# Graph layers in one kernel: a tile's own part of its mean added on TensorE, and eighteen instead of sixteen tiles that gather values together with keys

## The chip, the cores and the metric

The kernel runs on one core of one Trainium2 chip. A core has five engines with their own instruction streams: PE (TensorE: matrix products, which go to PSUM), DVE (VectorE), ACT (ScalarE), POOL (GpSimd) and SP (SyncE, which here only starts transfers). They meet through semaphores. Transfers that pick rows by a list of indices ("gathers") and transfers that write rows to listed places ("scatters") are issued by POOL; each picks one row of DRAM per partition. The metric is the device time of the whole kernel in microseconds.

## The reference

Two graph layers over 4096 nodes with 512 features and an adjacency matrix of 4096 x 4096 (about 0.2% ones, the diagonal set). Each layer is applied to the rectified layernorm of `x` and added to `x`:

```python
# layer 0: per head, the value of the neighbour with the highest score (hard attention)
attn = einsum('hqd,hkd->hqk', Q, K) * SCALING + (Q @ we.T + be)
attn = softmax(attn + where(adj > 0, 0, -inf))
hard = (attn == max(attn)) / HEADS
x = x + einsum('hqk,hkd->hqd', hard, V)
# layer 1: own part and mean over the neighbours
h = relu(layernorm(x))
agg = (adj > 0) @ h / max(deg, 1)
self_f, nb_f = h @ W_self + b_self, agg @ W_nb + b_nb
x = x + relu(concat([self_f, nb_f]) @ W_comb + b_comb)
```

A node is usually its own neighbour, so its own row is a part of the mean of layer 1: the row's product `h @ (W_nb W_comb)`, divided by the degree.

## The kernel before, in words

The rows are cut into 32 tiles of 128. The first part (to about 360 us) reads the adjacency, packs it into lists of neighbours, computes keys and values of all rows into one DRAM table `K_d` (a row holds value, key, meta data and x), and sorts the rows by degree; `perm` holds the order. After that tile 0 has the rows of highest degree (`CAPS[0]` = 24 neighbours) and tile 31 those of lowest (5).

The second part, the turns, goes over the tiles once. Two kinds of tile differ in how they get the values:

- an *apart* tile (`r < VTILE`) gathers only its neighbours' keys, into buffers `kg` (groups of four, four buffers), scores them on DVE (`scores`, a multiplication L1224 and a reduction L1227 for each group), finds the winner of each of the eight heads, and two or three turns later gathers the eight winning value pieces (`value_gathers`, 8 gathers, into `o`);
- a *fused* tile gathers key and value of a neighbour in one row twice as wide, into the big buffer `room`, and then takes the winning values out of `room` with one predicated copy for each neighbour (L1260).

The first group of `scores` is the row's own key, which came with its meta data. `room` is one region: `others(r)` gives the offset of a tile's neighbours, which is 0 for all fused tiles but two of the last four. The other half of `room` holds five slots for rows of fused tiles that fetch their whole own row (`wide`).

The order of turns is worked out by a small planner: four apart tiles first, the last three fused tiles last, and between them fused and apart tiles are mixed evenly. With `VTILE` = 16 these middle 25 turns are 13 fused and 12 apart tiles, which alternate strictly. The planner also fixes in which turn each later step of a tile is done: its values, its statistics (sum with x, L1289, and the normalisation on ACT, L1296 to L1323), its transposition, its two products on PE (`layer1`: `pg`, with the folded neighbour weights, and `pr`, with the folded own weights and the bias) and its move (`layer1_move`: `pg` to `gs` on ACT, L1360; `scatter` of `gs` to `G_d`). Five tiles are done at the end (`tail`) after the last turn.

All is issued in the order in which the loop over the turns writes it, each engine in order. In turn i POOL has: gathers of keys for turn i and values that are due, by turns, one of each; the row gather for turn i+5; the own values (if not wide); the scatter. ACT has: `layer1_move`, the copy of the query's transpose for turn i+2, the copy of the transpose for layer 1 (L1341), statistics, the query's norm for turn i+4, later the norm of layer 1. PE has: the query's product `q` for turn i+1 (L628), `layer1`, transpositions. On DVE `scores` calls `within` after the first gathered group: it takes a reciprocal (L1312) for the statistics that are under way, and does `layer1_out`: own row of the mean times reciprocal plus own product, a `scalar_tensor_tensor` (L1366), which SP stores to `X1_d`.

The third part sums the neighbours' rows of `G_d` (gathers into `room` and a reduction L1674 for 24 tiles; masks and matmuls L1652 for the 8 tiles of highest degree) and scatters the result to the output.

Of the kernel before, what the change touches and what calls it, by code (L numbers as in the profile page):

```python
# [9 lines left out]
F32 = mybir.dt.float32  # L10
BF16 = mybir.dt.bfloat16
I32 = mybir.dt.int32
AF = mybir.ActivationFunctionType
# [5 lines left out]
P = 128  # L19
D = 512  # L20
NC = D // P
H = 8
# [472 lines left out]
LIST = 24  # L495
# [4 lines left out]
M_DEG = 2 * LIST  # L500
M_LN = M_DEG + 1
M_RD = M_LN + 2
# [6 lines left out]
CAPS = (24, 15, 14, 13, 12, 12, 12, 11, 11, 11, 10, 10, 10, 10, 9, 9,  # L509
        9, 9, 9, 8, 8, 8, 8, 8, 7, 7, 7, 7, 6, 6, 6, 5)  # L510
GRP = 4
VTILE = 16
LISTV = CAPS[VTILE]
FIRST = 4
GMAX = 10
# [22 lines left out]
def sparse_path(  # L538
# [4 lines left out]
    nc = tc.nc  # L543
    N = x.shape[0]
    KT = N // P
# [8 lines left out]
    X1_d = dram.tile([N, 2, D], F32, tag="X1_d", name="X1_d")  # L554

    cp = ctx.enter_context(tc.tile_pool(name="sconst", bufs=1))
    ident = cp.tile([P, P], F32, tag="sid", name="sid")
    make_identity(nc, ident)
    identb = cp.tile([P, P], BF16, tag="sidb", name="sidb")
    beb = cp.tile([P, 1], F32, tag="sbe", name="sbe")  # L560
    hio = cp.tile([P, H], F32, tag="hio", name="hio")
    nc.gpsimd.iota(hio, [[1, H]], base=0, channel_multiplier=0, allow_small_or_imprecise_dtypes=True)
# [13 lines left out]
    smeta = cp.tile([P, KT, 8], F32, tag="smeta", name="smeta")  # L576
# [31 lines left out]
    def load_fold(k):  # L608
        nc.sync.dma_start(
            F[:, ds(2 * k * NC, NC), :],  # L610
            (wselfT, wnbT)[k].rearrange("(c p) f -> p c f", p=P),
        )
        nc.sync.dma_start(
            F[:, ds((2 * k + 1) * NC, NC), :],
            wcomb[ts(k, D), :].rearrange("(c p) f -> p c f", p=P),
        )
# [3 lines left out]
    def load_w(name, w, tag):  # L620
        t = wp.tile([P, NC, D], F32, tag=tag, name=name)
        nc.sync.dma_start(t, w.rearrange("(c p) f -> p c f", p=P))
        ws[name] = t


    def project(dst, h, w):
        for c in range(NC):
            nc.tensor.matmul(dst, h[:, c, :], w[:, c, :], start=(c == 0), stop=(c == NC - 1))  # L628

    with ExitStack() as pa:  # L630
        pa.enter_context(tc.manual_schedule())
        lp = pa.enter_context(tc.tile_pool(name="sl", bufs=1))
# [9 lines left out]
        st = [dict() for _ in range(KT)]  # L642
# [42 lines left out]
        load_adj(1)  # L685
        load_w("wv", wvT, "w_b")

        nc.vector.tensor_copy(identb, ident)

        planes = lp.tile([P, NPL, P], BF16, tag="planes", name="planes")  # L690
# [135 lines left out]
        def values(t, ps):  # L826
            pv = ps.tile([P, D], F32, tag="pm", name="pv")
            project(pv, hT(t), ws["wv"])
            return pv
# [100 lines left out]
        def on(step, t, *args):  # L930
            if 0 <= t < KT:
                step(t, *args)
# [159 lines left out]
    with ExitStack() as pb:  # L1092
        gp = pb.enter_context(tc.tile_pool(name="sg", bufs=4))
        bp = pb.enter_context(tc.tile_pool(name="sb", bufs=2))
# [37 lines left out]
        puts, last = [], [None]  # L1132
# [9 lines left out]
        st = [dict() for _ in range(KT)]  # L1142
# [75 lines left out]
        def scores(r, within):  # L1218

            s = st[r]  # L1220
            sc = bp.tile([P, LIST, H], F32, tag="sc", name="sc", bufs=1)
            for kk, g0, g in s["kg"]:
                pr = bp.tile([P, GRP, D], F32, tag="pr", name="pr", bufs=1)
                nc.vector.tensor_tensor(  # L1224
                    pr[:, :g, :], s["q"].unsqueeze(1).to_broadcast([P, g, D]), kk, ALU.mult
                )
                nc.vector.tensor_reduce(  # L1227
                    sc[:, g0 : g0 + g, :],
                    pr[:, :g, :].rearrange("p g (h d) -> p g h d", h=H), AX.X, ALU.add,
                )  # L1230
                if g0:
                    within()
                    within = lambda: None
            s["sc"] = sc
# [108 lines left out]
        def layer1(r):  # L1343
            s = st[r]
            s["pg"] = psm.tile([P, D], F32, tag="pm", name="pg")
            project(s["pg"], s["hT1"], wN)
            s["pr"] = own_product(s)

        def own_product(s):

            pr = psm.tile([P, D], F32, tag="pm", name="pr")
            nc.tensor.matmul(pr, ones[0:1, :], bb[0:1, :], start=True, stop=False)
            for c in range(NC):
                nc.tensor.matmul(pr, s["hT1"][:, c, :], wS[:, c, :], start=False, stop=(c == NC - 1))  # L1354
            return pr

        def layer1_move(r):
            s = st[r]
            s["gs"] = bp.tile([P, D], F32, tag="gs", name="gs")
            nc.scalar.copy(s["gs"], s["pg"])  # L1360

        def layer1_out(r):
            s = st[r]

            own = bp.tile([P, D], F32, tag="own", name="own")
            nc.vector.scalar_tensor_tensor(  # L1366
                own, s["gs"], smeta[:, r, M_RD + 1 - M_DEG : M_RD + 2 - M_DEG], s["pr"],
                ALU.mult, ALU.add,
            )
            nc.sync.dma_start(X1_d[ts(r, P), 1, :], own)  # L1370
# [6 lines left out]
        def load_bias():  # L1377
            for k in range(2):
                fb = bp.tile([P, D], F32, tag="own", name="fb")
                for c in range(NC):  # L1380
                    nc.vector.tensor_copy(
                        fb[:, ts(c, P)], bcs[k][:, c : c + 1].to_broadcast([P, P])
                    )
                fbs.append(fb)
# [47 lines left out]

        fused, apart = list(range(VTILE, KT)), list(range(VTILE))
        turns = apart[:FIRST]
# [23 lines left out]
        for r in turns:  # L1458
            p = pos[r]
# [7 lines left out]
        i = 0  # L1467
        while ready:
            ripe = sorted(e for e in ready if e[0] <= i)
            for e in ripe[: 2 if i >= KT - 4 else 1]:  # L1470
                ready.remove(e)
                r = e[2]
# [15 lines left out]
        def late(step, kind, i, *args):  # L1488

            out_ = []  # L1490
            for r in turns:
                if plan[kind].get(r) == i:
                    out_ += step(r, *args) or []
            return out_

        def tail_turn(r):

            k = tail.index(r)
            at = HALF_R + TAIL0 + k * D
            st[r]["hT1"] = room[:, at : at + D].rearrange("p (c q) -> p c q", q=P)  # L1500
            nc.scalar.copy(st[r]["hT1"], st[r]["hnp"])
# [15 lines left out]
        for i in range(-5, KT):  # L1517


            if i == -3:  # L1520
                load_fold(0)
            if i == 0:
                load_bias()
            if i == 1:
                wS = wp.tile([P, NC, D], F32, tag="w_b", name="swS")
                wN = bp.tile([P, NC, D], F32, tag="swN", name="swN", bufs=1)
            a, b = on(key_gathers, i), late(value_gathers, "value", i)
            while a or b:
                for q, n in ((a, max(1, round(len(a) / max(1, len(b))))), (b, 1)):
                    for g in q[:n]:  # L1530
                        gather(*g)
                    del q[:n]
            on(rows, i + 5)
            late(layer1_move, "move", i)
            on(query_copy, i + 2)
            late(layer1_copy, "layer1", i)
            early = [r for r in tail if plan["turn"][r] == i - 1]
            for r in early:
                tail_turn(r)
            if i >= 0 and turns[i] in fused:  # L1540
                own_values(turns[i])
            late(layer1_stats, "stats", i, i >= KT - 2)
            if i >= KT - 2:
                late(layer1_norm, "stats", i)
            on(query_norm, i + 4)
            on(query, i + 1)
            for part in between.get(i, ()):
                fold(*part)
            late(layer1, "layer1", i)
            for r in early:  # L1550
                tail_product(r)
            if i in (-2, -1, 0):
                n = 2
                for t in late_v[:n]:
                    w = values_out(t, values(t, psm), bp, nc.sync)
                    for g in beyond:
                        tc.declare_no_dep(w.ins, g.ins, reason="other columns")
                    written.append(w)
                del late_v[:n]
            if i == max(between) + 1:  # L1560
                fold_bias()

            def within():
                if i < KT - 2:
                    late(layer1_inverse, "stats", i)
                late(layer1_out, "move", i)

            if i >= 0:
                scores(turns[i], within)
            late(scatter, "move", i)  # L1570
            if i == KT - 2:
                wg = dense_words()
                gsl = [gp.tile([P, GRP, D], F32, tag="kg", name="gs") for _ in range(2)]
            on(winners, i)
            if i < KT - 2:
                late(layer1_norm, "stats", i)
            on(query_turn, i + 3)
            late(layer1_turn, "turn", i)
            for r in early:
                tail_move(r)  # L1580
# [10 lines left out]
            tail_move(r)  # L1591


        over = bp.tile([P, KT], F32, tag="over", name="over", bufs=1)
        r = 0
        while r < KT:
            e = r
# [5 lines left out]
            r = e  # L1603
# [11 lines left out]
        for r in tail:  # L1615
            s = st[r]
# [4 lines left out]
    with ExitStack() as pd:  # L1621
# [78 lines left out]
        s = ahead  # L1700
# [74 lines left out]
```

## Time and profile before

| | |
|---|---|
| median of 3 timed runs | 1424.04 us (1422.22 to 1430.38) |
| the profiled execution | 1295.04 us, span 1293.3 us |
| mean granted TensorE clock in it | 0.899 |
| first turn's scores begin on DVE | 362.8 us |
| last predicated copies begin on DVE | 966.3 us |
| last scatter to `G_d` | 985.7 us |
| DVE sums of `layer1_out` (L1366) | 32, 23.4 us, 733 ns each |
| predicated copies (L1260) | 102, 74.5 us, 731 ns each |
| value gathers into `o` by `vi` (POOL) | 128, 121.9 us, 952 ns each |

The columns of a timeline are the start in us, the duration in us, the engine, the line, the operation, what it writes and reads, how many instructions are merged into one row, and in brackets how long the engine was idle before and what ended that. In a table of stretches each engine has its busy time and, in brackets, its instructions; the last three columns are the granted TensorE clock, the share of DMA engines that were busy and the rate in GB/s. An instruction that only issues a transfer ends long before its data have landed.

### The profile page before, as it was taken

The numbers are of one execution on the slowest core, as the hardware profiler recorded it, in microseconds if no ns is written. First come the engines' busy times: TensorE is split into PE (matmuls) and PEld (weight loads), VectorE is DVE, ScalarE is ACT, GpSimd is POOL, SyncE is SP. The second block draws the span as 40 slices with busy tenths as digits, with TensorE's granted clock in tenths as the row PEclk, the third lists the DMA queues.
The fourth block names the chain that finished last, engine by engine and source line by source line (L and its number), as shares of the span: only waits on it lengthen the run. The fifth ranks groups of instructions, "written<-read, shape, count | busy, mean of one in ns | idle before, by whom it ended". The sixth has DMA issues, their size and how long they took to land.

```text
span 1293.3 us, 10762 instructions
## 1 busy us (share of the span) xinstructions
PE 1025.0 (79%) x2918; PEld 483.8 (37%) x2918; DVE 993.5 (77%) x1666; ACT 422.1 (33%) x862; POOL 776.3 (60%) x910
## 2 busy tenths in 40 slices
PE   5998998958779547767877887878798599999960
PEld 2555555523334213323333333333333244444420
DVE  5557777798279776889988889888792469788876
ACT  4778676831221222343434334344410000000000
POOL 2322323234477777777777777777553757777774
PEclk9999998988898868887889988988898799999985
DMA  9999998739585568888888888887753998888873
GB/s 358 419 421 420 418 420 306 274 133 379 194 253 165 157 186 238 270 265 263 262 264 257 256 249 264 262 246 240 270 187 119 307 356 274 281 271 274 279 248 119
DMA packets 109222, 350.09 MB, mean 271 GB/s; under 512 B 18064, under 2 KB 18064, under 8 KB 100960
## 3 DMA queue, kind: packets, MB, share of 16 engines
q0 software_dynamic: 63376, 208.23, 50.6%
q1 hardware_dynamic: 39552, 129.78, 25.9%
q10 hardware_dynamic: 6224, 11.31, 2.5%
q8 instruction: 25, 0.41, 0.1%
q14 instruction: 45, 0.37, 0.1%
HBM read 285.25 MB, written 68.19 MB: 273 GB/s over the span
## 4 chain that ended last, share of the span: by engine, by line
DVE 21%; DMA 21%; PE 20%; POOL 19%; issue 14%; ACT 3%; SPq 0%; DVEq 0%; POOLq 0%; ACTq 0%
POOL room L1103 9%; PE pv L628 6%; DMA room<-K_d,sidx 6%; DVE pr L1224 6%; DMA room<-G_d,sidx 5%; PE pk L628 5%; POOL kg L1103 5%; DMA kg<-K_d,sidx 4%; POOL o L1103 3%; DVE sc L1227 3%; PE pr L1354 2%; PE pw L768 2%; DMA adjt<-adj_dram 2%; ACT mkt L749 2%; PE pg L628 2%
## 5 line engine op out<-in xcount | busy, mean ns | idle before, releaser
L628 PE MATMUL q<-wq,hqT 128*128 128x512 f32 x256 | 161.2, 788 | 143.0 <-DVE pr L1224 143.0
L1652 PE MATMUL da<-gk,mk 128*128 128x512 f32 x512 | 221.4, 595 | 15.8 <-DMA gk<-G_d 15.8
L1103 POOL DMA_INDIRECT room<-G_d,sidx x174 | 180.3, 1036 | 58.0 <-issue 46.3
L1103 POOL DMA_INDIRECT kg<-K_d,sidx x177 | 169.6, 958 | 57.7 <-issue 45.0
L1227 DVE TENSOR_REDUCE sc<-pr 128x32 f32<-128x2048 f32 (+3 forms) x114 | 183.3, 1608 | 3.9
L1674 DVE TENSOR_REDUCE acc<-room 128x512 f32<-128x4096 f32 (+5 forms) x23 | 152.6, 6634 | 14.0 <-DMA room<-G_d,sidx 14.0
L1652 PEld LDWEIGHTS da<-gk,mk 128*128 128x128 f32 x512 | 97.8, 191 | 139.4 <-issue 139.0
L1103 POOL DMA_INDIRECT o<-K_d,vi x128 | 121.9, 952 | 39.0 <-issue 36.3
L628 PEld LDWEIGHTS q<-wq,hqT 128*128 128x128 f32 x256 | 62.5, 256 | 221.1 <-DVE pr L1224 124.2
L628 PE MATMUL pk<-wk,room 128*128 128x512 f32 x256 | 120.7, 616 | 3.6 <-ACT room L810 3.6
L1103 POOL DMA_INDIRECT room<-K_d,sidx x102 | 98.5, 966 | 31.5 <-issue 18.0
L628 PE MATMUL pv<-wv,room 128*128 128x512 f32 x256 | 115.9, 604 | 0.0
L1224 DVE TENSOR_TENSOR pr<-q,kg 128x2048 f32<-128x2048 f32 (+3 forms) x51 | 102.4, 2007 | 16.0 <-DMA kg<-K_d,sidx 14.4
L1224 DVE TENSOR_TENSOR pr<-q,room 128x2048 f32<-128x2048 f32 (+3 forms) x42 | 66.7, 1589 | 50.8 <-DMA room<-K_d,sidx 42.1
L1354 PE MATMUL pr<-swS,hT 128*128 128x512 f32 x216 | 99.9, 605 | 0.0
L628 PE MATMUL pg<-swN,hT 128*128 128x512 f32 x216 | 97.1, 592 | 0.0
L1296 ACT ACTIVATE hn<-xo 128x512 f32<-128x512 f32 x29 | 18.2, 629 | 192.6 <-DVE xo L1289 185.3
L824 POOL DMA_DIRECT2D K_d<-ks x32 | 18.7, 585 | 100.9 <-DVE ks L819 98.7
L749 ACT ACTIVATE mkt<-adjt,sgb 128x2048 bf16<-128x2048 int32 x37 | 74.2, 2006 | 13.1 <-POOL adjt L670 13.1
L1260 DVE COPY_PREDICATED o<-best,room 128x512 f32<-128x512 int32 x102 | 74.5, 731 | 3.5
L628 PEld LDWEIGHTS pv<-wv,room 128*128 128x128 f32 x256 | 49.6, 195 | 61.4 <-issue 61.2
L628 PEld LDWEIGHTS pk<-wk,room 128*128 128x128 f32 x256 | 48.3, 199 | 54.4 <-issue 48.8
(222 smaller groups left out, 1496.3 us busy)
## 6 DMA issues: line engine op xcount, KB each, us to landing
adjt<-adj_dram SPq DMA_DIRECT2D x37, 1024.0 KB, 11.2
room<-adj_dram SPq DMA_DIRECT2D x27, 1024.0 KB, 11.7
x<-X_d SPq DMA_DIRECT2D x32, 512.0 KB, 6.1
xt<-x_dram SPq DMA_DIRECT2D x32, 256.0 KB, 8.5
K_d<-ks POOLq DMA_DIRECT2D x32, 256.0 KB, 6.4
X_d<-xo SPq DMA_DIRECT2D x32, 256.0 KB, 4.0
X_d<-own SPq DMA_DIRECT2D x32, 256.0 KB, 3.9
gk<-G_d ACTq DMA_DIRECT2D x16, 512.0 KB, 6.0
```

Source lines behind the costliest of these rows:

```text
L628: nc.tensor.matmul(dst, h[:, c, :], w[:, c, :], start=(c == 0), stop=(c == NC - 1))
L749: nc.scalar.activation(mk, st[t]["adj"][j], AF.Sigmoid, bias=sgb, scale=400.0, accum_out=degs[:, t, j : j + 1],)
L768: nc.tensor.matmul(pw, planes[:, s, :], st[t]["mk"][j][:, ts(i, SEG)], start=False, stop=(s == NPL - 1),)
L824: nc.gpsimd.dma_start(K_d[ts(t, P), D : 2 * D], ks)
L1103: last[0] = nc.gpsimd.indirect_dma_start(out=dst, out_offset=None, in_=src, in_offset=bass.IndirectOffsetOnAxis(ap=idx, axis=0), element_o ...
L1224: nc.vector.tensor_tensor(pr[:, :g, :], s["q"].unsqueeze(1).to_broadcast([P, g, D]), kk, ALU.mult)
L1227: nc.vector.tensor_reduce(sc[:, g0 : g0 + g, :], pr[:, :g, :].rearrange("p g (h d) -> p g h d", h=H), AX.X, ALU.add,)
L1260: nc.vector.copy_predicated(s["o"].rearrange("p (h d) -> p h d", h=H), best[:, k, :].bitcast(I32).unsqueeze(2).to_broadcast([P, H, HD]), b ...
L1296: nc.scalar.activation(junk, xo, AF.Copy, scale=-1.0 / D, accum_out=q[:, 0:1])
L1354: nc.tensor.matmul(pr, s["hT1"][:, c, :], wS[:, c, :], start=False, stop=(c == NC - 1))
L1652: nc.tensor.matmul(dacc[r], masks[s][:, h, r, :], keys[s][:, h, :], start=(s == 0 and h == 0), stop=(s == NPL - 1 and h == 1),)
L1674: nc.vector.tensor_reduce(acc, g[:, 0:n, :].rearrange("p n f -> p f n"), AX.X, ALU.add)
```

## The change

For 27 of the 32 tiles the own part of the mean is no longer added on DVE. ACT makes a diagonal matrix `dg` (128 x 128) of the reciprocals of the degrees, by scaling the identity with one number per partition; PE multiplies `dg` with `gs` and adds the product to the group `pr`, which is left open for that; ACT copies the finished sum out of PSUM, and SP stores it. The five tiles of the end keep the sum on DVE. The diagonal and the matmul are done in the turn of the tile's move: `dg` on ACT after the copy of the transpose and ahead of the statistics, the matmul on PE ahead of `q`, the copy on ACT after the scores. `dg` has one buffer.

`VTILE` is 14 instead of 16: tiles 14 and 15 (nine neighbours with the row itself) become fused. The middle 25 turns are then 15 fused and 10 apart tiles, in the order (from turn 5) 14, 5, 15, 16, 6, 17, 7, 18, 19, 8, 20, 9, 21, 22, 10, 23, 11, 24, 25, 12, 26, 13, 27; before it was 16, 5, 17, 6, 18, 7, 19, 8, and so on to 15, 27.

The bf16 identity moves to a pool that is freed after the first part, and the buffer `over` of the last check takes the place of the scores `sc`.

```diff
-VTILE = 16
+VTILE = 14
...
-            s["pr"] = own_product(s)
+            s["pr"] = own_product(s, False)
...
-        def own_product(s):
+        def own_product(s, last=True):
             pr = psm.tile([P, D], F32, tag="pm", name="pr")
             nc.tensor.matmul(pr, ones[0:1, :], bb[0:1, :], start=True, stop=False)
             for c in range(NC):
-                nc.tensor.matmul(pr, s["hT1"][:, c, :], wS[:, c, :], start=False, stop=(c == NC - 1))
+                nc.tensor.matmul(
+                    pr, s["hT1"][:, c, :], wS[:, c, :], start=False, stop=last and c == NC - 1
+                )
             return pr
...
+        def layer1_diag(r):
+            s = st[r]
+            s["dg"] = bp.tile([P, P], F32, tag="dg", name="dg", bufs=1)
+            nc.scalar.activation(
+                s["dg"], ident, AF.Copy, scale=smeta[:, r, M_RD + 1 - M_DEG : M_RD + 2 - M_DEG]
+            )
+
+        def layer1_mean(r):
+            s = st[r]
+            nc.tensor.matmul(s["pr"], s["dg"], s["gs"], start=False, stop=True)
+
+        def layer1_own(r):
+            s = st[r]
+            own = bp.tile([P, D], F32, tag="own", name="own")
+            nc.scalar.copy(own, s["pr"])
+            nc.sync.dma_start(X1_d[ts(r, P), 1, :], own)
...
             for r in early:
                 tail_turn(r)
+            late(layer1_diag, "move", i)
             if i >= 0 and turns[i] in fused:
                 own_values(turns[i])
             late(layer1_stats, "stats", i, i >= KT - 2)
...
             on(query_norm, i + 4)
+            late(layer1_mean, "move", i)
             on(query, i + 1)
...
                     late(layer1_inverse, "stats", i)
-                late(layer1_out, "move", i)
 
             if i >= 0:
                 scores(turns[i], within)
+            late(layer1_own, "move", i)
             late(scatter, "move", i)
...
-        over = bp.tile([P, KT], F32, tag="over", name="over", bufs=1)
+        over = bp.tile([P, LIST, H], F32, tag="sc", name="over", bufs=1).rearrange(
+            "p s h -> p (s h)"
+        )[:, 0:KT]
```

More of the change, by code (lines that the diff above doesn't have):

```diff
@@ L558, in sparse_path @@
     make_identity(nc, ident)
-    identb = cp.tile([P, P], BF16, tag="sidb", name="sidb")
     beb = cp.tile([P, 1], F32, tag="sbe", name="sbe")
@@ L686, in sparse_path @@
         load_w("wv", wvT, "w_b")
+        identb = lp.tile([P, P], BF16, tag="sidb", name="sidb")
         nc.vector.tensor_copy(identb, ident)
```

## The prediction

> **What bounds the kernel now.** I read the page's busy table first, then the engines by stretch of time, then the timelines of POOL and DVE, last the chain that ended last.
>
> ```profile
> PE 1025.0 (79%) x2918; PEld 483.8 (37%) x2918; DVE 993.5 (77%) x1666; ACT 422.1 (33%) x862; POOL 776.3 (60%) x910
> ...
> 600.00:720.00 120.00, 90.61 (x220) 39.94 (x220) 109.87 (x135) 47.09 (x122) 90.79 (x95) 0.87 0.84 262
> 720.00:840.00 120.00, 100.16 (x249) 43.80 (x249) 106.35 (x136) 47.14 (x122) 91.19 (x95) 0.91 0.82 258
> ```
>
> No engine is full over the span. The change lives in the turns, 360 to 960 us. There (columns: PE, PEld, DVE, ACT, POOL busy) POOL looks 76% busy, but it issued 95 instructions in 120 us: 1.26 us from start to start, which is what a gather costs (0.95 busy, 0.31 "issue"). POOL never pauses from 380 to 880 us: it sets the pace. DVE, at 90%, is next.
>
> ```profile
> 610.11 0.95 POOL L1103 DMA_INDIRECT room<-K_d,sidx  x1 [0.30 <-issue]
> ...
> 615.13 0.99 POOL L1119 DMA_INDIRECT G_d<-gs,perm  x1 [0.30 <-issue]
> ...
> 616.25 1.75 DVE L1224 TENSOR_TENSOR pr<-q,room 128x1536 f32<-128x1536 f32 x1
> 616.42 0.97 POOL L1103 DMA_INDIRECT kg<-K_d,sidx  x1 [0.30 <-issue]
> ...
> 620.71 5.33 DVE L1260 COPY_PREDICATED o<-best,room 128x512 f32<-128x512 int32 x7
> ```
>
> Turn 11, a fused one: its last key gather starts at 610.11, DVE can multiply at 616.25, and its copies, which read the values out of room, begin at 620.71. POOL goes on to the next turn's gathers at 616.42, since an apart tile gathers into kg. The first copy ends at 621.47: a next tile that needed room would have waited 5.0 us.
>
> After the turns the chain leaves POOL for PE:
>
> ```profile
> 914.34 6.70 PE L628 MATMUL q<-wq,hqT 128*128 128x512 f32 x8 [4.21 <-DVE pr L1224]
> ...
> 917.06 0.56 ACT L1360 COPY gs<-pg 128x512 f32<-128x512 f32 x1
> 917.52 0.59 ACT L1173 COPY hqT<-tr 128x512 f32<-128x512 f32 x1
> 918.00 0.60 ACT L1341 COPY hT<-tr 128x512 f32<-128x512 f32 x1
> ...
> 933.05 5.40 PE L628 MATMUL q<-wq,hqT 128*128 128x512 f32 x8 [3.02 <-DVE pr L1224]
> ...
> 935.65 0.56 ACT L1360 COPY gs<-pg 128x512 f32<-128x512 f32 x1
> 936.11 1.07 ACT L1341 COPY hT<-tr 128x512 f32<-128x512 f32 x2
> ```
>
> The chain of waits runs q 914.34, pg 921.04, pr, transpose, ACT statistics, DVE, q 933.05, and on to 954.68 on PE. Here q starts before that iteration's gs and hT are copied.
>
> [...] eight q records take 6.70 us after 4.21 idle and 3.60 when PE was busy. [...] the trace's 128x128 activation with a pointer bias, L758, took 0.391.
>
> **The change part by part.** Sums are against the profiled execution: 1295.04 us, span 1293.3. The timed runs have a median of 1424.04, 10% above it, and no view shows where those 129 us lie; I add the difference in us to the median.
>
> *DVE.* 27 of the 32 sums own L1366 leave DVE: 27 x 0.733 = -19.8. Two more fused tiles of nine keys add 16 predicated copies at 0.76 = +12.2 and drop half of two winner selections, -2.0. DVE net -9.6, worth nothing by itself while POOL sets the pace.
>
> *POOL.* Tiles 14 and 15 lose 8 value gathers each: 16 x 1.26 = -20.2. The gathers of own values stay five; key gathers keep their number and double in width (+4.2 MB, -0.5 MB, under DMA engines 84% busy).
>
> *The order of turns.* Before, fused and apart turns alternate. With 18 fused, 15 of the middle 25 turns are fused, so fused follows fused at turns 7-8, 12-13, 17-18 and 22-23. Both write room from its start, so the first key gather of the second waits on POOL for the first predicated copy of the first. Value gathers, row gathers and the scatter queue behind it. The wait can be read off the trace before, as first copy end less POOL's next first kg: 5.7 in turn 7, 8.0 in turn 9 (eight keys); 5.0, 4.5, 4.2 in turns 11, 13, 15 (seven); 1.9 and 2.3 in turns 21 and 23 (six). For the pairs: 5.7 + 7 + 4.6 + 2.3 = 19.6.
>
> That assumes DVE as far behind POOL as today. Between pairs it falls back: value gathers bunch in the pairs and the turns between have none. Take time 0 at turn 8's first key. POOL issues 18 + 13 + 10 + 12 and reaches turn 12 at 66.8. DVE's second group of turn 8 lands at 17.6 + 5.9 (as in turns 5 to 9), its scores and copies end at 35.2; turns 9, 10, 11 take 16.9, 18.3, 15.8 (from 2.29 per multiply or reduction of four keys, 0.76 per copy): 86.2. With own row (2.0) and first group (4.6), turn 12's second group starts at 92.9, where its keys landed at 90.3: 2.6 late, all of it added to the wait. The same sums give 2 and 4 for turns 17 and 22: there DVE needs 15.8 + 15.5 + 15.8 and 14.7 + 14.5 + 14.7 for the three turns between, and POOL, without value gathers, 41 and 39 us or less. Waits: 20 to 29; less 20.2: 0 to +9. A gather that lands sooner because POOL paused before would pull toward the low end, so I take +6.
>
> *PE and ACT in the turns.* The trace has no such mean matmul: nearest are two warm fp32 records of q, 0.90, and the bias matmul's two, 1.05 on the chain (L1352); right after idle two records take up to 1.9, but then q behind it takes less. I take 1.05: 27 x 1.05 = 28 us of PE, and 27 x (0.39 + 0.57) = 26 us of ACT. Mean stands on PE before q, and waits for gs and dg, so q now waits for ACT's gs, hqT, hT, dg. Cover: DVE wants q only one turn (15 to 20 us) after q could start. PE per turn is 1.05 + 3.6 + 3.6 + 4.7 + 1.0 = 14.0, plus 1.7 of ACT ahead and some 2 of cold clock: 17.7, about the mean turn (15 turns from 626.52 to 882.96: 17.1), with that one turn in hand. I charge nothing in the middle; without the cover each turn would pay up to 1.05. The sums' stores stay on SP, which is idle. pr's bank comes free no later: ACT copies it soon after the turn's statistics, where DVE's sum came after the first group.
>
> *PE and ACT at the end.* In turns of 12 and 9 us that cover is gone. Iteration 29: dg is ready at 919.0, mean ends 920.15, and q starts there instead of 914.34: +5.8, carried by pg, pr, transposes and statistics. Iteration 30: dg at 937.6, q at 938.7 instead of 933.05: +5.6. Iteration 31 has two means and one dg buffer: dg, mean, dg stand on ACT ahead of the square root that DVE waits for: +2.0. The two DVE sums at 964.22 on the chain go: -1.4. Together +12; bounds -2 (all hidden) and +14. I take +11. Everything after the last scatter (985.67) shifts with it; the last stage is unchanged.
>
> The moved bf16 identity and the shared buffer of over cost nothing: one-off, and at the end DVE has long finished with sc.
>
> Sum: -20.2 + 26 + 11 = +17: 1312 profiled, 1441 as a median.
>
> **The rivals.** (a) *Handovers short, end hidden: faster.* It decides at four waits totalling 20.2. The six-key turns (2 us) speak for it, the eight-key turns (5.7 to 8.0) against. At 12 us of waits and -2 at the end: -10, 1414. (b) *End hidden, middle as forecast*: q not on the chain in the last turns, because POOL's gathers come later. For: DVE waits for gathers at 908 and 924. Against: the chain is on PE from 914 to 955. +6 - 2 = +4: 1428. (c) *PE becomes the bound of all turns*, by cold clock and the wait for dg: PE's 17.7 against turns of 15.5 between the pairs; if every one of 27 turns pays 1.05, +28 more: 1469. Against it: the 14 us of slack before q is wanted.
>
> **How the numbers follow.** Forecast 0.55, (b) 0.18, (a) 0.15, (c) 0.12. About 0.5%, 7 us, is what a measurement here can tell from no change. Faster takes most of (a), 0.15; same most of (b) and an edge of the forecast, 0.16; slower 0.69. The likeliest one's own range is 1431 to 1452. The range 1416 to 1459 leaves out the low end of (a) and most of (c).
>
> **What would show it.** POOL's room gathers waiting for DVE's o L1260, 4 to 10 us, four times, at turns 8, 13, 18, 23, and nowhere else. POOL 16 instructions fewer at 1.26. PE's first record before each q waiting for ACT dg; in the last turns q starting after hT's copy, and from the last first-key gather of turn 27 to the last scatter some 11 us more. DVE's idle time before pr up although its busy time falls by 10. Wrong if the waits sum below 15, or if the stretch after 880 is no longer than before; or if the timed runs' extra 129 us lie in a stage that the change touches.

## The result and the profile after

The kernel after took 1492.9 us in the median of six runs (1475.1 to 1511.3), the kernel before 1429.5 beside it (six runs, 1422.2 to 1449.6): a ratio of 1.0393, 95% interval 1.035 to 1.0436, so some 63 us slower where 17 were forecast. The sign was right and the size was not. Medians here are over all runs of a kernel; ratios are over its faster runs alone, those within 1.5% of its fastest, so the two can differ a little.

The page of the kernel after, its busy line and the groups that changed most (busy time and mean of one, then the engine's idle time before the group and what ended it):

```profile
PE 1058.2 (72%) x2972; PEld 493.4 (33%) x2972; DVE 987.5 (67%) x1647; ACT 444.3 (30%) x918; POOL 759.7 (52%) x894
...
L1374 PE MATMUL pr<-gs,dg 128*128 128x512 f32 x54 | 40.8, 846 | 202.8 <-ACT dg L1367 146.1
...
L1103 POOL DMA_INDIRECT room<-K_d,sidx x118 | 114.0, 966 | 86.4 <-DVE o L1260 52.3
...
L1119 POOL DMA_INDIRECT G_d<-gs,perm x32 | 32.8, 1026 | 136.1 <-ACT gs L1362 102.7
...
L1312 DVE RECIPROCAL q<-q 128x1 f32<-128x1 f32 x29 | 4.6, 159 | 111.8 <-ACT q L1298 86.7
```

POOL has its 16 instructions fewer and waits at the handovers, as forecast, but for 52 us and not 20 to 29. What no step of the forecast had: the row scatter G_d waits 102.7 us for gs (8.8 in the trace of the prediction), and DVE waits 86.7 us for ACT's square root in the middle of its scores (2.9 there). The same two stretches of the turns that the prediction showed, by engine (columns: length, then PE, PEld, DVE, ACT and POOL busy, the granted clock, the DMA share, GB/s):

```profile
600.00:720.00 120.00, 64.45 (x164) 28.55 (x163) 81.26 (x95) 38.15 (x98) 63.30 (x66) 0.79 0.63 200
720.00:840.00 120.00, 80.55 (x205) 35.23 (x203) 86.55 (x98) 40.12 (x103) 75.02 (x79) 0.84 0.74 232
```

POOL, which issued 95 instructions in 120 us in the prediction's trace, issues 66 in the first stretch, and DVE falls from 110 us to 81. Part of this is not the change: a trace of the kernel before that is as long as its timed runs (the first experiment below) has for the first stretch

```profile
600.00:720.00 120.00, 82.88 (x190) 34.31 (x189) 93.96 (x116) 38.41 (x101) 79.89 (x83) 0.79 0.75 227
```

so 83 instructions of POOL and 94 us of DVE, and in that trace the scatter waits 76.2 us for gs and DVE 49.5 for the square root. In the kernel after all engines stand still for part of the time. One such stop, in its timeline (from 1019.80, the end of POOL's last gather, to 1023.18 it has no engine at work):

```profile
999.83 0.60 PE L1138 MATMUL tr<-sid,hq 128*128 128x128 f32 x4
...
1000.26 0.60 PE L1138 MATMUL tr<-sid,hn 128*128 128x128 f32 x4
...
1001.93 2.29 DVE L1227 TENSOR_REDUCE sc<-pr 128x32 f32<-128x2048 f32 x1
...
1018.85 0.95 POOL L1103 DMA_INDIRECT o<-K_d,vi  x1 [0.30 <-issue]
1023.18 0.58 ACT L1173 COPY hqT<-tr 128x512 f32<-128x512 f32 x1 [26.82 <-remote]
1024.60 0.58 ACT L1341 COPY hT<-tr 128x512 f32<-128x512 f32 x1 [0.84 <-remote]
1025.08 0.40 ACT L1367 ACTIVATE dg<-sid,smeta 128x128 f32<-128x128 f32 x1
...
1025.54 2.07 PE L1374 MATMUL pr<-gs,dg 128*128 128x512 f32 x2 [24.68 <-ACT dg L1367]
...
1027.82 0.16 DVE L1312 RECIPROCAL q<-q 128x1 f32<-128x1 f32 x1 [23.61 <-ACT q L1298]
...
1036.14 1.15 POOL L1119 DMA_INDIRECT G_d<-gs,perm  x1 [16.34 <-ACT gs L1362]
```

By their records the eight transposes were over at 1000.86; the copy that needs them began 22 us later. Behind that copy stand, on ACT, hT, the diagonal and the square root that DVE wants; on PE the mean and q; on POOL the scatter. "Remote" means that the trace has no record of what ended the wait, so that the wait was for PE is read from what the copy needs.

One thing has to be said for these numbers to be understood: the trace shown before the prediction (1295 us) comes from a condition without such stops, and the timed runs (1424 to 1430 for the kernel before) from one with them. The experiments met both, at different times also on one and the same chip, so it isn't a property of a chip. Below, "with stops" and "without stops" name the two conditions; each kernel is compared only with the kernel before that ran beside it.

### The profile page after: what moved, and what is told of

Same layout as the page of the kernel before. It is cut to its first block, busy times and chain, and to the rows that moved or that the text cites. A ratio compares the mean times of both kernels' runs of the same rounds, so it can differ in the third digit from the quotient of the medians.

```text
span 1472.9 us, 10869 instructions
## 1 busy us (share of the span) xinstructions
PE 1058.2 (72%) x2972; PEld 493.4 (33%) x2972; DVE 987.5 (67%) x1647; ACT 444.3 (30%) x918; POOL 759.7 (52%) x894
## 5 line engine op out<-in xcount | busy, mean ns | idle before, releaser
L1676 PE MATMUL da<-gk,mk 128*128 128x512 f32 x512 | 234.8, 617 | 37.8 <-issue 21.4
L1103 POOL DMA_INDIRECT kg<-K_d,sidx x161 | 154.6, 960 | 71.8 <-issue 48.3
L1374 PE MATMUL pr<-gs,dg 128*128 128x512 f32 x54 | 40.8, 846 | 202.8 <-ACT dg L1367 146.1
L627 PE MATMUL q<-wq,hqT 128*128 128x512 f32 x256 | 138.3, 690 | 30.1 <-issue 29.6
L1103 POOL DMA_INDIRECT room<-K_d,sidx x118 | 114.0, 966 | 86.4 <-DVE o L1260 52.3
L1103 POOL DMA_INDIRECT o<-K_d,vi x112 | 107.1, 957 | 34.3 <-issue 33.8
L1224 DVE TENSOR_TENSOR pr<-q,room 128x2048 f32<-128x2048 f32 (+3 forms) x48 | 77.3, 1611 | 38.8 <-DMA room<-K_d,sidx 22.2
L1119 POOL DMA_INDIRECT G_d<-gs,perm x32 | 32.8, 1026 | 136.1 <-ACT gs L1362 102.7
L1260 DVE COPY_PREDICATED o<-best,room 128x512 f32<-128x512 int32 x118 | 86.0, 729 | 6.5 <-issue 1.3
L1374 PEld LDWEIGHTS pr<-gs,dg 128*128 128x128 f32 x54 | 10.3, 238 | 209.8 <-ACT dg L1367 151.7
L1312 DVE RECIPROCAL q<-q 128x1 f32<-128x1 f32 x29 | 4.6, 159 | 111.8 <-ACT q L1298 86.7
```

Source lines behind the costliest of these rows:

```text
L1103: last[0] = nc.gpsimd.indirect_dma_start(out=dst, out_offset=None, in_=src, in_offset=bass.IndirectOffsetOnAxis(ap=idx, axis=0), element_o ...
L1119: new = nc.gpsimd.indirect_dma_start(out=dst, out_offset=bass.IndirectOffsetOnAxis(ap=perm[:, r : r + 1], axis=0), in_=src, in_offset=None,)
L1224: nc.vector.tensor_tensor(pr[:, :g, :], s["q"].unsqueeze(1).to_broadcast([P, g, D]), kk, ALU.mult)
L1260: nc.vector.copy_predicated(s["o"].rearrange("p (h d) -> p h d", h=H), best[:, k, :].bitcast(I32).unsqueeze(2).to_broadcast([P, H, HD]), b ...
L1374: nc.tensor.matmul(s["pr"], s["dg"], s["gs"], start=False, stop=True)
L1676: nc.tensor.matmul(dacc[r], masks[s][:, h, r, :], keys[s][:, h, :], start=(s == 0 and h == 0), stop=(s == NPL - 1 and h == 1),)
```

## The experiments

### The kernel before, once more, for its trace with stops

No edit.

> The kernel before, unchanged, for a trace of an execution as long as its timed ones. Theory D (whatever makes the timed runs 130 us longer than the first profile is not in the changed stage alone): median 1420 to 1435, and this trace shows PE standing still for 10 to 25 us at a time in the folding of the weights (turns 1 to 3, +40 us) and in the last stage (+50 us), like the trace after. Rival (the first profile stands for the timed runs): the same span as the first profile within 1%, no such stops.

1435.7 us beside 1433.0 for the same kernel (ratio 0.9987, 0.9954 to 1.002), span 1428.7. Its trace has the stops: in the folding of the weights (turn 3 starts at 477.3 instead of 433.1), in every second turn, and in the last stage. Of the 135 us by which it is longer than the prediction's trace, 44 have come by turn 3, 56 more by the last row scatter (1085.8 instead of 985.7), and 35 in the last stage, where 50 were expected. One of the stops, in its timeline:

```profile
648.34 3.70 PE L628 MATMUL pg<-swN,hT 128*128 128x512 f32 x8 [0.45 <-issue]
...
657.44 1.02 PE L628 MATMUL q<-wq,hqT 128*128 128x512 f32 x2
...
660.38 0.59 PE L628 MATMUL q<-wq,hqT 128*128 128x512 f32 x1 [1.92 <-issue]
...
663.21 1.01 PE L628 MATMUL q<-wq,hqT 128*128 128x512 f32 x1 [2.24 <-issue]
...
666.73 1.01 PE L628 MATMUL q<-wq,hqT 128*128 128x512 f32 x1 [2.52 <-issue]
...
668.84 1.01 PE L628 MATMUL q<-wq,hqT 128*128 128x512 f32 x1 [1.10 <-issue]
...
673.03 1.01 PE L628 MATMUL q<-wq,hqT 128*128 128x512 f32 x1 [1.07 <-issue]
673.12 0.59 ACT L1360 COPY gs<-pg 128x512 f32<-128x512 f32 x1 [19.27 <-remote]
...
676.51 0.16 DVE L1312 RECIPROCAL q<-q 128x1 f32<-128x1 f32 x1 [2.99 <-ACT q L1298]
```

This is what a stop looks like here: PE's matmuls, otherwise 0.43 us apart, start 2.1 to 3.5 us apart for some 16 us while they wait for nothing that the profile shows ("issue"), and ACT gets on with gs only when that is over. POOL's gathers keep their 1.26 us until the scatter needs gs. The records can't be read to the end, though. The pg that gs copies was over at 652.04 by its record, ahead of the slow stretch, and in the stop of the kernel after no slow matmul is recorded at all. So either PE is behind its own records, or its signals reach the other engines late; the traces don't tell which, and "stop" stands for either. Nor can it be read from PE's records which instruction a stop falls on; what can be read is which instruction of ACT waits. Here it is gs, and behind it comes little that is urgent: after 19 us of waiting on ACT, DVE has waited 2.99 for its statistics.

### Each half of the change alone, with stops

Eighteen fused tiles, with the mean still summed by DVE:

```
-VTILE = 16
+VTILE = 14
```

(and the two buffer moves of the change).

> Eighteen fused tiles, the mean still summed by DVE (with the identity and the sharing of the buffer as in the kernel after). Theory H (the handovers carry the loss): the four waits of POOL were 51.7 us in the trace after, less 20.2 of gathers: +25 to +35 us, ratio 1.018 to 1.025. Theory M (the mean in front of q carries it): within 7 us of the kernel before, waits of POOL at the four handovers 20 to 29 us in all.

1442.0 beside 1433.0, ratio 1.0071 (1.004 to 1.0102): +9 us. Theory H, that the handovers carry the loss, falls. Theory M has the time nearly right and the waits wrong: POOL waits 50.2 us for DVE's copies, not 20 to 29, so with stops these waits don't add up to lost time. It ran again later, also with stops:

> Eighteen fused tiles with the mean on DVE. Without PE's slow stretches: handovers 20 to 29 us less 20.2 of gathers, 0 to +9 us, ratio 1.000 to 1.007. With them: +9 us, ratio 1.007, as in its first run.

1445.6 beside 1430.8, with 1428.5 to 1470.5 in four runs: +15, no more than the same order of size (POOL's waits for the copies 41.1). In both traces ACT meets stops at hqT (73.3 and 92.5 us), although no mean stands on PE.

The mean on TensorE, with sixteen fused tiles:

```
-VTILE = 14
+VTILE = 16
```

(in the kernel after).

> The mean by TensorE, sixteen fused tiles as before. Theory M: q waits in every turn for ACT's gs, hqT, hT and dg, so a late PE is a late ACT and a late PE again: +30 to +60 us, ratio 1.02 to 1.04, and PE waits for dg above 100 us as after. Theory H: +11 us from the last turns alone, ratio 1.008, PE waits for dg below 60 us.

1555.9 beside 1433.0: +123 us, twice the loss of the whole change and twice what theory M had expected at most. So the mean carries the loss, and fusing two more tiles takes part of it back.

### The order on PE, with stops

```
-            late(layer1_mean, "move", i)
             on(query, i + 1)
+            late(layer1_mean, "move", i)
```

> The kernel after with the mean issued on PE behind q instead of in front of it. Theory M: 25 to 45 us back, 1450 to 1468 us, DVE's waits for the statistics fall from 87 us to under 40. Theory H: as the kernel after, 1485 to 1495.

In the kernel after: 1475.6 beside 1433.0, ratio 1.0205 (1.0113 to 1.0297). By the medians it gives back some 15 to 20 us, less than theory M wanted; by the ratios 1.9 points, about 27 us. Four runs can't decide between the two. DVE's wait for its statistics is 73.8 us in the trace, not under 40, and ACT still waits 130.1 at hqT. The same edit with sixteen fused tiles ran first without stops:

> Sixteen fused tiles, the mean on TensorE but behind q. Theory L: as with the mean in front, 1535 to 1560. Theory W: q waits for hqT alone again, 1440 to 1480, and PE's waits for dg fall from 256 us to under 80.

There it took 1301.3 beside 1294.7, +6.6 us (ratio 1.0057, 1.0038 to 1.0076), which says nothing on the question asked. Later, with stops, it ran beside the mean in front of q:

> Sixteen fused tiles, the mean on TensorE in front of q. Beside 1295: +6 to +13 us, as its sisters (no bias +6, early diagonal +13), since q has a turn in hand. Beside 1430: +115 to +130 us again; one matmul more alone gave +12, the mean without the bias +20, so a result below +60 would say that the first one was chance.

> Sixteen fused tiles, the mean behind q. Beside 1295: +6 us as measured. Beside 1430, theory P (a slow stretch that falls on the eight transposes holds hqT, hence dg, the mean, q and ACT's square roots one behind the other): 60 us or more back from the +123, so +10 to +60. Theory L (the number of PE's instructions alone): +110 or more.

Mean in front of q: 1510.5 beside 1427.0, +83 us (ratio 1.0673, with a wide interval, 1.0252 to 1.1095), less than the +115 to +130 expected. Mean behind q: 1439.9, +13 us (1.0193, 1.0007 to 1.0379), as theory P had it. The two kernels have the same instructions, and only the place of 27 means on PE differs: in these runs the order alone is worth 70 us, and the four runs of one (1437 to 1449) lie clear of the four of the other (1497 to 1531). The answers on waits show where (total, times, longest). The mean in front of q:

```profile
ACT hqT L1173 <- remote: 132.8, 10, 23.2
DVE q L1312 <- ACT q L1298: 115.3, 11, 20.8
```

The same view of the mean behind q:

```profile
ACT own L1379 <- remote: 181.5, 10, 21.3
DVE q L1312 <- ACT q L1298: 55.2, 15, 10.3
...
PE pr L1374 <- ACT dg L1367: 15.5, 15, 2.4
```

And of the kernel before, with stops:

```profile
ACT gs L1360 <- remote: 153.7, 9, 20.0
...
DVE q L1312 <- ACT q L1298: 49.5, 13, 10.1
```

Each has long waits of ACT, 130 to 180 us in its largest group. In front of q, ACT meets most of them at hqT, ahead of all that DVE and PE want next, and DVE waits 115 us for its statistics (232.1 and 225.1 in the first run, which took 1556). Behind q, ACT meets them at the copy of own values, the last of its work in an iteration, and DVE waits 55, as in the kernel before (49.5).

All twelve traces with stops go with this reading, though that doesn't prove it. DVE's wait for its statistics is 44 to 55 us in the four executions of 1430 to 1444 us (the kernel before, the fused tiles alone twice, the mean behind q with sixteen), 74 to 157 in the seven of 1475 to 1504, and 225 in the one of 1550. The kernel after, beside these two:

> The kernel after again. If the kernel before takes about 1295 us beside it: the forecast's working says +10 to +25 us, with POOL's four waits at the handovers 20 to 29 us; rival: +8 us or less, waits below 15. If it takes about 1430: +55 to +60 us again.

1490.1 beside 1427.0, +63 us (1.0544, 1.0361 to 1.0728). ACT waits 117.1 us at hqT and DVE 114.8 at the reciprocal.

### Is it PE's load?

The rival to the order was the number of PE's instructions. One more matmul per tile in the kernel before, which adds zeros (`zrow` is a tile of zeros; the two buffer moves are in it too):

```
             nc.tensor.matmul(pr, ones[0:1, :], bb[0:1, :], start=True, stop=False)
+            nc.tensor.matmul(pr, zrow, wS[:, 0, :], start=False, stop=False)
```

and the mean in front of q without the bias matmul (its line taken out, so that PE has as many as before). Both ran first without stops:

> The kernel before, with one more matmul per tile of the same size as the mean's (a stationary of zeros, so it adds nothing) inside the own product: the mean's PE load without its operands, its place or ACT's two operations. Theory L (PE's load: in the timed runs PE falls into stretches of 15 to 25 us in which its matmuls start 1.4 to 2.8 us apart, and more load brings more of them): +60 to +120 us, 1490 to 1555. Theory W (q waits behind the mean for ACT's diagonal): within 15 us of the kernel before.

> Sixteen fused tiles, the mean on TensorE in front of q, and the bias matmul of each tile left out (the bias is missing from the output), so that PE has as many matmuls as before. Theory L: 1425 to 1455. Theory W: 1535 to 1560, since the wait for dg is untouched.

1301.6 and 1301.2 beside 1294.7: +6.9 and +6.4 us (1.0051, 1.0034 to 1.0068, and 1.0048, 1.0033 to 1.0063). Theory L speaks of the condition with stops, which these runs can't judge. They ran again with them:

> The kernel before with one more matmul per tile and nothing else. Without the slow stretches +7 us as measured. With them: theory L (load brings more stretches) +60 to +120 us; theory W (the wait for dg and the place of the mean cost the time) +7 to +20 us.

> Sixteen fused tiles, the mean in front of q, the bias matmul left out. Without the slow stretches +6 us as measured. With them: theory L within 20 us of the kernel before; theory W +100 us or more.

One more matmul: 1442.5 beside 1430.8, ratio 1.0072 (1.0019 to 1.0126), +12 us. The mean without the bias: 1450.4, +20, with 1420.5 to 1489.0 in four runs. Theory L in its simple form falls (it wanted +60 or more for the first), but so does theory W (+100 or more for the second). These two kernels don't hold one time: the first took 1426 to 1445 in eight executions and 1462 to 1505 in five. Its profiled one took 1504, and there ACT waits 252.4 us at hqT, though no mean stands on PE. So where the stops fall is not fixed by the order alone. With as many instructions as before, or with the order of before, they sometimes fall badly, so PE's load isn't excluded as a part of the cause; with both changed, all eight runs of the mean in front of q lay above 1496.

### The diagonal made earlier

The diagonal issued right behind gs, ahead of hqT and hT (except in iteration 31, where two tiles share one buffer):

```
             late(layer1_move, "move", i)
+            if i < KT - 1:
+                late(layer1_diag, "move", i)
             on(query_copy, i + 2)
...
```

> Sixteen fused tiles, the mean on TensorE in front of q, the diagonal made right after gs and ahead of hqT and hT, so that the mean no longer waits for hT and dg behind it. Theory L: 1535 to 1560. Theory W: half or more of the 123 us back, 1440 to 1495.

> Sixteen fused tiles, the mean in front of q, the diagonal made ahead of hqT and hT. Beside 1295: +13 us as measured. Beside 1430: if the wait for ACT's diagonal is what turns a slow stretch into lost time, +10 to +50; if it is the place in front of q, +80 to +125 as with the late diagonal.

Both runs were without stops: 1308.2 beside 1294.7 (1.0104, 1.0074 to 1.0134) and 1308.6 beside 1292.9 (1.0103, 1.0058 to 1.0149), +13 and +16. Whether the wait for the diagonal or the mean's place in front of q matters with stops was not measured.

### The kernel after without stops

A first run for it met stops again:

> The kernel after, unchanged. There are two conditions by now: in one the kernel before takes about 1430 us with PE's slow stretches, in the other 1295 us without them. Without them, the forecast's own working holds: +10 to +25 us over the kernel before (1305 to 1320), POOL's waits at the four handovers 20 to 29 us. With them: +55 to +65 us, 1480 to 1500, as first timed. Rival to the forecast: without them no more than +8 us, the handovers below 15 us.

1487.4 beside 1430.8, +57 us (1.0407, 1.0293 to 1.0522). The last one was without them:

> The kernel after once more. Beside a kernel before of 1295 us: +10 to +25 us by the forecast's working, POOL's four waits 20 to 29 us; rival: +8 us or less. Beside 1430: +57 to +63 us, as three times before.

> Sixteen fused tiles, the mean in front of q. Beside 1295: +6 to +13 us. Beside 1430: +80 to +125 us, as twice before.

The kernel after: 1309.9 beside 1292.9, ratio 1.0120 (1.0076 to 1.0165): +17.0 us. The mean alone: 1313.0, +20.1 (1.0138, 1.0088 to 1.0188), more than the +6 to +13 expected. The forecast's sum, made on a trace without stops, was +17; the mean's share in it was +11 and that of the two fused tiles +6.

## Why the size was wrong, and what was right

**The step that failed** is in the part on the sums: "The timed runs have a median of 1424.04, 10% above it, and no view shows where those 129 us lie; I add the difference in us to the median." Adding them so takes the 129 us to lie beside the change. They don't: they come with stops, and in the kernel before 56 of 135 us lie in the turns, in the order of work that the change edits. The price of the change there is +57 to +63 and not +17. The prediction named this as what would make it wrong, and gave it no case in its range.

With stops, a second step goes with it: "I charge nothing in the middle", for which the cover was the one turn by which q is ahead. ACT's longest wait in a trace with stops is 20 to 35 us, as long as that turn of 15 to 20 or longer. From DVE's first own row to its own row of turn 29 the timelines give 644.2 us for the kernel before with stops, and 685.0, 688.0 and 705.7 in three traces of the kernel after, +41 to +61 where +6 was charged; from there to the last row scatter they differ by +8. Rival (c), that PE becomes the bound of the turns, is the nearest in kind, but it had cold clock (the granted clock is 0.54 from 914 to 921 us of the prediction's trace, after 4.21 us of idle time, and 0.98 from 905 to 914) and 1.05 us per turn for its mechanism and +28 for its price, and the runs show waits of another kind, at ACT's hqT and behind it.

**Without stops every large term held.** The handovers, in POOL's timeline of the kernel after:

```profile
545.88 0.97 POOL L1103 DMA_INDIRECT room<-K_d,sidx  x1 [6.28 <-DVE o L1260]
...
645.02 0.97 POOL L1103 DMA_INDIRECT room<-K_d,sidx  x1 [9.15 <-DVE o L1260]
...
735.70 0.97 POOL L1103 DMA_INDIRECT room<-K_d,sidx  x1 [5.58 <-DVE o L1260]
...
822.32 0.97 POOL L1103 DMA_INDIRECT room<-K_d,sidx  x1 [5.74 <-DVE o L1260]
```

Four waits, 26.8 us together; 20 to 29 were forecast and 26 taken. At the own row of turn 29 the kernel is 4.1 us behind (924.8 against 920.7; forecast 6). The middle turns, from the waits of the same run:

```profile
PE pr L1374 <- ACT dg L1367: 99.1, 27, 14.1
...
PE q L627 <- DVE pr L1224: 47.0, 13, 17.4
...
DVE q L1312 <- ACT q L1298: 7.2, 1, 7.2
```

PE waits for each of the 27 diagonals (0.416 us each on ACT, where 0.39 was taken), as forecast, and pays with idle time that it had: its waits for DVE fall from 143.0 to 47.0 us, and DVE waits for ACT's square root once. That is the cover that the prediction named, at work, and mostly used up. The end, in PE's timeline:

```profile
923.62 2.08 PE L1374 MATMUL pr<-gs,dg 128*128 128x512 f32 x2 [4.93 <-ACT dg L1367]
925.49 4.29 PE L627 MATMUL q<-wq,hqT 128*128 128x512 f32 x8
...
946.75 2.07 PE L1374 MATMUL pr<-gs,dg 128*128 128x512 f32 x2 [7.98 <-ACT dg L1367]
948.61 4.67 PE L627 MATMUL q<-wq,hqT 128*128 128x512 f32 x8
```

q starts at 925.49 and 948.61, where it started at 914.34 and 933.05: 11.2 and 15.6 later, or 7.1 and 11.5 after the 4.1 of the middle; forecast 5.8 and 11.4. The mean takes 2.08 there, after 4.93 and 7.98 us of idle time, and not 1.05; after 1.02 us of idle time, at 1056.40 in the first trace of the kernel after (span 1472.9), it takes 1.13. The last row scatter is 16.1 us later (1001.76 against 985.67), 12.0 of it at the end; forecast 11. The spans differ by 14.6 and the medians by 17.0.

That the sum met the median to the microsecond is in part luck. The mean alone costs as much as the whole change (+20.1 beside +17.0, with intervals that overlap); in its trace the last row scatter is 15.5 us late, 1.4 of it by turn 29 and 14.1 at the end, where 0 and 11 were charged. So the two more fused tiles add 0.6 us there and not 6: the mean was priced about 4 us too low and the fused tiles about 5 too high. The fused tiles alone did not run without stops.

**What stays open.** What causes the stops, and what decides on which of PE's instructions one falls, no run shows. The order moves it (70 us between the mean in front of q and behind it with sixteen fused tiles, 15 to 27 with eighteen), and so do the number of instructions and the pattern of the turns (two more fused tiles turn +83 to +123 into +57 to +63), but that these act through where the stop falls is read from the waits and was not set by an experiment. By the answers on waits POOL waits for DVE's copies 45.8 to 52.3 us in the kernel after with stops and 27.4 without; that a stop which met DVE ahead of its copies makes the difference is likely and not shown.

One rival stands untested: the recording itself. Up to 340 us all the traces hold nearly the same number of semaphore events, 4933 to 4952, and up to there the two traces of the kernel before stay within 3 us of each other. From 360 us on, where the stops are, the traces with stops hold 4139 to 5096 such events and those without 14106 to 14431, for nearly the same instructions. Whether the missing records and the stops have one cause, or one brings the other, no run shows. The waits that end with "remote" go with it: the prediction's trace has none.

No version here beats the kernel before in either condition. The nearest that moves the mean is the one behind q with sixteen fused tiles, +6.6 and +13 us.

## What to carry to other kernels

If the profiled execution and the timed runs differ by 10%, as here with 1295 and 1424 us, the profile need not stand for the timed runs: get a trace as long as the timed runs before a change is priced, or let the range take in what the missing time may do in the changed stage, and look whether both traces hold as many semaphore events. On a queue that serves two others, a wait in front of work that was ahead cost little here as long as no single delay was longer than that lead (without stops, where PE's longest wait for a diagonal was 8.0 us, the mean in front of q cost 1.4 us by turn 29; with stops, where ACT's longest waits were 20 to 35 us beside a lead of 15 to 20, it cost +83 and +123 us in all). So put the new, unhurried work (here the mean) behind the hurried: with stops that gave back 70 us with sixteen fused tiles and 15 to 27 with eighteen. And a term that is hidden should be stated with how much cover is left afterwards: here 47 us of PE's waits out of 143.

## What the runs showed of the hardware

In the records of some executions TensorE's fp32 matmuls of 128x512 start 2.1 to 3.5 us apart instead of 0.43, for some 16 us in the stretch shown, with no wait in the trace, while gathers keep their 1.26 us. The granted clock doesn't explain it: in the stretch from 658 to 672 us of the kernel before its mean is 0.63. In the prediction's trace it is 0.54 from 914 to 921 us, and the eight matmuls of q that run there after idle time, 6.70 us in all, start some 0.9 apart. What makes the spacing five to eight times as wide, no run shows.

At two starts of PE after idle time in the prediction's trace the granted clock is low and then full: 0.54 from 914 to 921 us (4.21 us idle before) and 1.00 from 921 to 929, 0.69 from 933 to 938.5 (3.02 idle before) and 1.00 from 938.5 to 946. In the turns of that trace eight matmuls of q take 5.15 to 6.72 us in the 19 cases in which PE was idle for 2.62 us or more before them, and 3.60 to 3.70 where it was idle for 1.80 or less.

The same program on the same chip took 1430 us at one time and 1293 at another. In the first stage, up to 240 us, where PE is busy 84 to 92% of the time, the two traces of the kernel before agree within about 1% of PE's busy time, so a busy PE alone doesn't bring the stops on.
